# Two-layer network on one core: where the second batch's routing stands in the order against the first batch's last layers

## Chip, cores and metric

The kernel runs on one core of a Trainium2 chip. The metric is the device time of one execution, in microseconds; lower is better. The kernel before took 4369.77 us, the median of three executions (4367.19 to 4371.41).

## What is computed

Four batches of 384 channels by 32 x 32 pixels (1024 tokens) go through two layers, all in float32. Layer 0 is a selective scan in four directions (a recurrence over the tokens with 16 states for each channel), then a mixture of experts: each token picks two of four FFNs of 384 to 1536 to 384. Layer 1 is attention with eight heads and shared q, k and v, then an FFN with Kronecker-structured weights. Cut to what matters:

```python
x = x + scan(ln_c(x))                 # layer 0: four directions, 16 states
t = tokens(x)
t = t + moe(ln_t(t))                  # softmax gate, top 2 of 4 experts
x = from_tokens(t)
x = x + attention(ln_c(x))            # layer 1: softmax(w w^T) w, projection out
t = tokens(x)
t = t + gelu(ln_t(t) @ w_fc.T) @ w_proj.T   # w_fc, w_proj: kron of small matrices
return from_tokens(t)
```

Batches do not depend on each other.

## The kernel before

**Scan.** `scan_layer` walks over 32 units: for each of four batches, four directions, and in each two halves of 512 tokens. `project` prepares the next unit (x_proj, dt, softplus) while `chunk` computes the current one. A unit has three channel blocks `c` of 128 channels, and each four groups `g` of states: 12 steps. In a step POOL multiplies dt*u by B into `bx` (L438, twice) and one half of h by C (L466), ACT computes exp(dt*A) into `da` (L447, four times), DVE runs the recurrence (L452, four times) and multiplies the other half by C (L459, twice), and PE sums the states into the PSUM tile `acc` (L473, four matmuls, each of which the profile counts twice). `bx` has six buffers of which a step takes two; `dtr`, loaded by SP (L422), has seven. At the end of a batch `finish` normalises, applies Gelu, adds the input (POOL, L235) and stores `x1[b]`.

**Tail.** Everything behind the scan is done batch by batch. `between(b)` is called when the scan of batch b has been emitted, and emits `tail_batch(b - 1)`; batch 3 has its tail after the scan. A tail consists of
- `route` and `spread`: load x1, transpose and score it on PE (`tt_ps`, L654), copy (ACT, L640), statistics (DVE, L641, L660, L661), store it as tokens, then `places`: some 60 small DVE instructions that rank the experts and give every token two rows (its counting matmuls at L751 and L752); then the tokens are loaded again, normalised, and scattered with 16 indirect DMAs from POOL's queue (L681) into `rows`, which `clear` has filled with zeros;
- `experts`: 11 slots of gathered rows, each with a load of weights (L869 to L881), a gather (`xs`, L897), transposes (`xc_ps`, L908, copied by DVE at L912), and two products (L925, L940);
- `combine` and `prologue`: 16 indirect gathers on POOL (L970), gate weights, residual, layer norm;
- `attention`: s_ps (L1049), exp on ACT (L1055), o_acc (L1095), and a division by the sums at the end (L1063 to L1076);
- `last_layers`: loads wa, wb, wc and xt (L1119 to L1135), adds the bias on POOL (L1136), projects out into `o_ps` (L1142; DVE L1145 to L1147 add it, and form the FFN's small input), transposes that (`z_ps`, L1164), runs the FFN (`h_ps` L1180, Gelu L1189, `f_acc` L1197) and stores `out` (L1217).

**Order.** A scheduler puts the emitted instructions of each engine into one fixed order at build time, by priority (the order of emission) and a timeline of its own. Blocks under `high_priority(offset=FORWARD)` are taken as if they had been emitted 20,000 instructions earlier, so that they slip between the scan's instructions. `last_layers` and `spread` are such blocks; `attention` and `experts` are not. In the tail of batch b, `second_layer` is given a function that emits the routing of batch b + 1. Tails share one `Room` of buffers: `k4` (five), `kw` (eight), `k12` (two), and four PSUM banks (`o` one, `p` three). On the machine each engine takes its instructions in this order, and waits on semaphores.

Of the kernel before, what the change touches and what calls it, by code (L numbers as in the profile page):

```python
# [114 lines left out]
class Body:  # L115
# [393 lines left out]

    def second_layer(self, b, xc, room, between):  # L510
        att = self.attention(xc, self.sums[:, b], room)
        between()
        with self.tc.high_priority(offset=FORWARD):
            self.last_layers(b, att, room)

    def overflow(self, room):

        nc = self.nc
        flag = self.const.tile([1, 1], I32, tag="flag", name="flag")
        top = room.tile([P, 1], "top", "top")  # L520
        nc.vector.tensor_reduce(
            top, self.sums.rearrange("p b t m i -> p (b t m i)"), AX.X, ALU.max
        )
        ps = room.bank("p", "top_ps")
        nc.tensor.matmul(ps[:1, :P], top, self.ident, start=True, stop=True)
        nc.vector.tensor_reduce(top[:1, :], ps[:1, :P], AX.X, ALU.max)
        nc.vector.tensor_scalar(flag, top[:1, :], LIMIT, None, op0=ALU.is_gt)
        return flag
# [925 lines left out]
```

## Time and profile before

| | |
|---|---|
| median of three executions | 4369.77 us |
| the profiled execution | 4344.16 us, span 4342.4 us |
| granted TensorE clock, mean | 0.857 |
| POOL busy | 3049.3 us (70%) |
| PE busy | 3303.7 us (76%) |
| DVE busy | 2915.6 us (67%) |
| ACT busy | 2504.3 us (58%) |
| DMA engines, mean rate | 160 GB/s |
| POOL's last scan multiply ends | 3487.4 us |

How to read it: the profile lists the busy time of each engine as a share of the span, and cuts the span into forty equal slices whose busy share is given in tenths (9 stands for 90% or more; PEclk is the clock that TensorE was granted). The times by stage give, for a stretch of time, each engine's busy us and, in brackets, its number of instructions. In a group of instructions the columns are busy time and the mean ns of one, then the engine's idle time before them and what ended it. In a wait, the columns are total us, times, and the longest one. "L473" is a line of the kernel before.

### The profile page before, as it was taken

The numbers are of one execution on the slowest core, as the hardware profiler recorded it, in microseconds if no ns is written. First come the engines' busy times: TensorE is split into PE (matmuls) and PEld (weight loads), VectorE is DVE, ScalarE is ACT, GpSimd is POOL, SyncE is SP. The second block draws the span as 40 slices with busy tenths as digits, with TensorE's granted clock in tenths as the row PEclk, the third lists the DMA queues.
The fourth block names the chain that finished last, engine by engine and source line by source line (L and its number), as shares of the span: only waits on it lengthen the run. The fifth ranks groups of instructions, "written<-read, shape, count | busy, mean of one in ns | idle before, by whom it ended". The sixth has DMA issues, their size and how long they took to land. (4 is left out here: it accounts for less than half of the span.)

```text
span 4342.4 us, 45822 instructions
## 1 busy us (share of the span) xinstructions
PE 3303.7 (76%) x13340; PEld 1577.5 (36%) x13340; DVE 2915.6 (67%) x4331; ACT 2504.3 (58%) x4460; POOL 3049.3 (70%) x1475
## 2 busy tenths in 40 slices
PE   6444454398987885679986887569987889998896
PEld 2111111155552222245553222235554235666323
DVE  5999997887787868878886778967877730200101
ACT  5555555466665775467665776466665664343353
POOL 5999997798888968789998688778988820000100
PEclk8666666599998996789998999779998899999897
DMA  5444564567795535458888434457789443335200
GB/s 142 129 119 127 142 160 120 180 196 233 220 281 151 151 118 147 145 161 241 228 242 246 137 107 124 136 149 223 214 237 268 121 147 107 116 127 210 64 17 16
DMA packets 410131, 694.49 MB, mean 160 GB/s; under 512 B 50832, under 2 KB 209424, under 8 KB 409872
## 3 DMA queue, kind: packets, MB, share of 16 engines
q1 hardware_dynamic: 400560, 665.07, 53.6%
q0 software_dynamic: 8192, 25.17, 1.8%
q8 instruction: 107, 1.75, 0.2%
q14 instruction: 152, 1.25, 0.1%
q10 hardware_dynamic: 1120, 1.24, 0.1%
HBM read 569.79 MB, written 121.50 MB: 159 GB/s over the span
## 5 line engine op out<-in xcount | busy, mean ns | idle before, releaser
L438 POOL TENSOR_TENSOR bx<-dtr,bcs 128x1024 f32<-128x1024 f32 x768 | 1795.1, 2364 | 216.2 <-PE acc L473 103.2
L447 ACT ACTIVATE da<-dtr,nega 128x512 f32<-128x512 f32 x1536 | 1045.2, 690 | 994.2 <-DVE bx L459 628.9
L466 POOL TENSOR_TENSOR bx<-bx,bcs 128x1024 f32<-128x1024 f32 x384 | 905.2, 2362 | 160.3 <-DVE carry L463 67.3
L473 PE MATMUL acc<-bx,sel 128*32 128x512 f32 x3072 | 499.2, 702 | 342.4 <-POOL bx L466 273.7
L925 PE MATMUL h_ps<-xc,w 128*128 128x256 f32 (+1 forms) x3168 | 659.5, 363 | 52.0 <-DMA w<-in_w 27.0
L940 PE MATMUL y_ps<-w,hs 128*128 128x384 f32 x1824 | 649.6, 509 | 57.5 <-ACT hs L933 43.6
L925 PEld LDWEIGHTS h_ps<-xc,w 128*128 128x128 f32 x3168 | 547.6, 196 | 219.9 <-issue 92.3
L452 DVE TENSOR_TENSOR_SCAN bx<-da,carry,bx 128x512 f32<-128x512 f32 x384 | 474.0, 1269 | 140.4 <-POOL bx L438 79.5
L452 DVE TENSOR_TENSOR_SCAN bx<-da,bx 128x512 f32<-128x512 f32 x384 | 453.2, 1210 | 107.7 <-ACT da L447 61.7
L452 DVE TENSOR_TENSOR_SCAN da<-da,carry,bx 128x512 f32<-128x512 f32 x384 | 476.9, 1274 | 62.7 <-ACT da L447 51.8
L459 DVE TENSOR_TENSOR bx<-da,bcs 128x512 f32<-128x512 f32 x768 | 509.5, 679 | 3.1
L452 DVE TENSOR_TENSOR_SCAN da<-da,bx 128x512 f32<-128x512 f32 x384 | 455.7, 1219 | 76.0 <-ACT da L447 54.9
L940 PEld LDWEIGHTS y_ps<-w,hs 128*128 128x128 f32 x1824 | 353.6, 198 | 346.0 <-issue 75.7
L1055 ACT ACTIVATE ex<-s_ps 128x512 f32<-128x512 f32 x512 | 300.1, 590 | 157.1 <-PE s_ps L1049 156.1
L1049 PE MATMUL s_ps<-w 64*128 64x512 f32 x1024 | 309.9, 666 | 54.5 <-ACT ex L1055 53.8
L1095 PE MATMUL o_acc<-ex,vt 128*64 128x512 f32 x1024 | 285.6, 637 | 32.9 <-ACT ex L1055 23.5
L473 PEld LDWEIGHTS acc<-bx,sel 128*32 128x32 f32 x3072 | 77.0, 116 | 640.9 <-POOL bx L466 386.6
L930 ACT ACTIVATE hs<-h_ps,bb 128x256 f32<-128x256 f32 (+1 forms) x528 | 199.9, 439 | 185.3 <-PE h_ps L925 180.6
L961 POOL TENSOR_TENSOR diag<-ident,g_weight 128x1024 f32<-128x1024 f32 x8 | 15.1, 1899 | 326.9 <-DMA w<-in_w 312.1
L944 DVE TENSOR_TENSOR y<-y_ps,bb 128x384 f32<-128x384 f32 x76 | 41.7, 549 | 259.0 <-PE y_ps L940 259.0
L363 PE MATMUL dt_ps<-xd,wdt 108*128 108x512 f32 x192 | 123.9, 732 | 73.3 <-ACT mag L402 43.9
L1049 PEld LDWEIGHTS s_ps<-w 64*128 64x128 f32 x1024 | 83.5, 192 | 254.2 <-ACT ex L1055 202.3
(214 smaller groups left out, 3688.4 us busy)
## 6 DMA issues: line engine op xcount, KB each, us to landing
w<-in_w SPq DMA_DIRECT2D x352, 576.0 KB
dtr<-dd SPq DMA_DIRECT2D x1536, 128.0 KB
bcs<-both SPq DMA_DIRECT2D x512, 128.0 KB
dd<-one_e SPq DMA_DIRECT2D x96, 256.0 KB
dd<-mag SPq DMA_DIRECT2D x96, 256.0 KB
rows<-zero SPq DMA_DIRECT2D x76, 192.0 KB
xs<-rows SPq DMA_DIRECT2D x32, 384.0 KB
made<-y SPq DMA_DIRECT2D x32, 384.0 KB
```

Source lines behind the costliest of these rows:

```text
L438: pool = nc.gpsimd.tensor_mul(bx, dtr[q][1], bc[:, 0].unsqueeze(1).to_broadcast([P, 2, HF])).ins
L447: nc.scalar.activation(da, dtr[q][0][:, j, :], AF.Exp, scale=nega[:, col : col + 1])
L452: nc.vector.tensor_tensor_scan(run(h), run(da), run(bx[:, j, :]), 0.0 if first else hold, ALU.mult, ALU.add,)
L459: dve = nc.vector.tensor_mul(bx[:, j, :], h, cg).ins
L466: pool = nc.gpsimd.tensor_mul(bx, bx, cg.unsqueeze(1).to_broadcast([P, 2, HF])).ins
L473: nc.tensor.matmul(acc[lo : lo + DB, :], sel, out[q][:, j, :], start=(g == 0), stop=(g == NG - 1),)
L925: nc.tensor.matmul(ps[:, r, :], w1[(f + r) // wf][:, c, (f + r) % wf * P : ((f + r) % wf + 1) * P], xc[:, c, :], start=(c == 0), stop=(c = ...
L930: nc.scalar.activation(hs[:, f + r, :], ps[:, r, :], AF.Identity, bias=bb[:, f + r : f + r + 1])
L940: nc.tensor.matmul(out[:, :D], hs[:, f, t * P : (t + 1) * P], w2[f // wf][:, f % wf, :], start=(f == 0), stop=(f == FC - 1),)
L1049: ins = nc.tensor.matmul(ps, w[rows, j * P : (j + 1) * P], w[rows, halves(i)], start=True, stop=True).ins
L1055: done.append(nc.scalar.activation(ex[:, o, :], ps, AF.Exp, scale=HD**-0.5, accum_out=sums[:, t, 2 * j + o, i : i + 1],).ins)
L1095: ins = nc.tensor.matmul(out[cols, :], made[t][1][:, j, cols], ex[:, o, :], start=(j == 0), stop=(j == MB - 1),).ins
```

## The change

In `second_layer`, for the first batch alone, the call that emits the second batch's routing is put behind `last_layers` of the first batch; for the other batches it stays ahead of it.

```diff
     def second_layer(self, b, xc, room, between):
         att = self.attention(xc, self.sums[:, b], room)
-        between()
+        if b > 0:
+            between()
         with self.tc.high_priority(offset=FORWARD):
             self.last_layers(b, att, room)
+        if b == 0:
+            between()
```

`between` is the function that `tail_batch` passes. It calls `route(1, ...)` for b = 0, `route(2, ...)` for b = 1 and nothing for b = 2; for batch 3 it is empty. No instruction is added or taken away. Behind the edit each line of the kernel has a number higher by three.

## Prediction

> **What bounds the kernel now.** I read the page first (busy shares, then the forty slices), then the busy times by stage, then the waits of single engines in the stages that the change touches.
>
> ```profile
> PE 3303.7 (76%) x13340; PEld 1577.5 (36%) x13340; DVE 2915.6 (67%) x4331; ACT 2504.3 (58%) x4460; POOL 3049.3 (70%) x1475
> PE   6444454398987885679986887569987889998896
> DVE  5999997887787868878886778967877730200101
> POOL 5999997798888968789998688778988820000100
> PEclk8666666599998996789998999779998899999897
> ```
>
> There are two regimes. Up to about slice 32 (3487 us, where POOL's last scan multiply ends) POOL and DVE share the scan and are both at 7 to 9 tenths. After it PE alone is full: the last batch's layers and the rest of the third's. The chain of waits that ends last lies wholly in that second part, so the time is the end of the scan plus about 855 us. The change touches neither the scan's work nor the end's; it can only move the end of the scan, or the amount of tail work left behind it.
>
> I cut the scan into its 32 units (batch, direction, half), each ending with POOL's 36th multiply, and each unit into 12 steps of four sums into acc. The change bears on units 16, 17 and 18 (steps 180 to 216). The busy times by stage, in order: these three, four undisturbed units under expert work, the regime after the scan:
>
> ```profile
> core 0: us, PE busy (x) PEld busy (x) DVE busy (x) ACT busy (x) POOL busy (x), PEclk, DMA share, GB/s
> 1517.70:1653.30 135.60, 110.80 (x452) 33.85 (x448) 97.24 (x124) 94.56 (x211) 99.17 (x44) 0.91 0.42 125
> 1653.30:1774.60 121.30, 68.01 (x220) 28.94 (x220) 108.21 (x217) 59.53 (x96) 97.17 (x48) 0.71 0.47 130
> 1774.60:1900.20 125.60, 73.58 (x300) 27.44 (x300) 92.04 (x128) 82.14 (x115) 106.61 (x60) 0.68 0.47 149
> 1900.20:2301.20 401.00, 370.94 (x1647) 232.62 (x1648) 338.47 (x458) 268.94 (x427) 364.33 (x170) 0.97 0.85 237
> 3487.00:4342.00 855.00, 763.92 (x3199) 398.10 (x3197) 111.21 (x298) 369.52 (x784) 51.93 (x40) 0.93 0.31 102
> ```
>
> An undisturbed unit takes 401.0 / 4 = 100.25 us. Our three take 382.5, so 82 us hang on the batch boundary, the routing and the last layers. In the second DVE is the bound (108.2 of 121.3), in the third POOL (106.6, the scatter's 16 indirect DMAs among it). PE has half its time free: that PE's order moves is worth nothing by itself; what counts is where DVE's small work lies, and who stands in a queue behind a late wait.
>
> **What the Trainium skill says.** PSUM — Partial Sum Buffer, "Engine vs sequencer instructions": matmuls start and complete in program order, and the queues of ScalarE, VectorE and GpSimdE are strict FIFO. The trace agrees: PE stood 12.5 us before z_ps (L1164) for DVE's z, with sums of the scan behind it. SBUF — State Buffer, "Who interferes with whom": a DVE instruction with two SBUF inputs contends with a GpSimd instruction that reads SBUF, and the one that comes second blocks. The trace shows this strongly. The same 128x32 addition, in the first batch's routing (beside a busy POOL) and in the second's (beside a POOL that waits for DVE):
>
> ```profile
> L665 DVE TENSOR_TENSOR sc<-sc,bg 128x32 f32<-128x32 f32 x1 | 2.3, 2273 | 0.0
> ...
> L665 DVE TENSOR_TENSOR sc<-sc,bg 128x32 f32<-128x32 f32 x1 | 0.2, 182 | 0.0
> ```
>
> **The change, part by part.** No instruction is added or removed. The built order of instructions (it carries no times) shows what moves.
>
> *Projection out and FFN go forward.* The eight o_ps groups stood at steps 199 to 202 on PE and now stand at 187 to 191; the FFN ends at step 203 instead of 212. Its loads wa, wb (step 191 of SP) and wc (195) keep their place, and so does POOL's 6.7 us addition L1136 (step 187); only its six stores of out go forward on SP, from 215-219 to 204-211. On DVE one group is these four, plus 0.16 for its statistics:
>
> ```profile
> L1146 DVE TENSOR_TENSOR o_ps<-xt,wb 128x384 f32<-128x384 f32 x8 | 9.4, 1180 | 0.0
> L541 DVE BATCH_NORM_STATS2 st<-xt 128x6 f32<-128x384 f32 x8 | 4.4, 547 | 0.0
> L1145 DVE TENSOR_TENSOR xt<-xt,o_ps 128x384 f32<-128x384 f32 x8 | 4.3, 534 | 0.3 <-PE o_ps L1142 0.3
> L1147 DVE TENSOR_REDUCE zt<-o_ps 128x32 f32<-128x384 f32 x8 | 4.3, 533 | 0.0
> ```
>
> That is 1.18 + 0.55 + 0.53 + 0.53 + 0.16 = 2.95 us a group. Five of eight groups now fall before step 192: 14.8 us more for DVE in unit 16, less 3.5 for four tiles of routing (L641, L660, L661: 0.86 each) that leave: +11.3. Is there room?
>
> ```profile
> 1625.00:1653.30 28.30, 15.12 (x86) 7.82 (x86) 26.54 (x41) 16.09 (x28) 24.63 (x11) 0.75 0.52 158
> 1653.30:1700.00 46.70, 25.07 (x78) 8.61 (x79) 38.27 (x63) 26.27 (x39) 45.27 (x23) 0.65 0.61 157
> 1700.00:1774.60 74.60, 42.94 (x144) 20.33 (x143) 69.94 (x155) 33.26 (x57) 51.90 (x26) 0.75 0.38 113
> ```
>
> In the last 28.3 us of unit 16 DVE is busy for 26.5 (finish's layer norm lies there), so no: I take +11 for unit 16 (bounds 0, if it fits into DVE's 38 idle us earlier in the unit, and +15). Unit 17 loses those 14.8 and 9.7 of routing and gains some 6 of z and fc1's copy: DVE 108.2 - 24.5 + 6 = 90. The three groups left (8.9) lie in 1653-1700, where DVE has 8.4 free. POOL's 97.2 becomes the bound; with the idle share of an undisturbed unit (POOL 364.3 of 401.0, 9%) that is 107, with PE's stop at z_ps, which stays, 110: -11 (bounds -21, the undisturbed pace, and 0). ACT's Gelu and copies (33 us) go into a unit where ACT is busy for 59.5 of 121: nothing.
>
> *Routing goes back.* Its transposes move from steps 187-196 to 204-205, its two counting matmuls from 199 to 208, its 75 small DVE instructions from 198-206 to 208-211.5, and its scatter on POOL from 206.67 to 212.33. Its four loads and four stores of x (384 KB each) and four loads of xt now stand at 211-212 on SP, behind the stores of out; SP's dtr loads behind them have seven buffers and run about five steps ahead, so I cost this at nothing (bound: one dtr load late, 8 us). The clearing of rows (19 stores, step 175) stays. Now the expert stage's first gather, xc_ps, stands at 212.5 on PE and 213 on DVE, directly behind the scatter; before, seven steps lay between. This form exists in the trace: in the first batch the scatter is at 105.67, xc_ps at 105 and a block of 32 h_ps at 106. That unit shows its price:
>
> ```profile
> 753.40:886.30 132.90, 53.99 (x189) 24.90 (x190) 106.47 (x211) 59.75 (x97) 109.75 (x62) 0.61 0.58 182
> ...
> DVE xc L912 <- PE xc_ps L908: 19.4, 1, 19.4
> ...
> PE xc_ps L908 <- DMA xs<-rows: 16.1, 1, 16.1
> ```
>
> DVE stands 19.4 us at the copy of xc with the scan's instructions behind it, and PE 16.1 for the gathered rows with acc behind it. In unit 18 of before the corresponding waits are 11.1 on PE and 4.5 on DVE. Routing is dearer on DVE, too: 29.0 us in that unit (the groups of its lines summed), 18.9 in the second batch. So unit 18 goes from 125.6 to that unit's 132.9: +7 (bounds -5, if the last layers that leave take more with them, and +20).
>
> *Afterwards.* Expert work starts at step 213 instead of 214, the second batch's attention ends at 295 instead of 300, the third's experts start at 316 instead of 319, but the third's attention starts at step 371 in both. Behind the scan stand 190 matmuls of it instead of 194: four s_ps or o_acc of 0.53 us, -2.
>
> Sum: +11 - 11 + 7 - 2 = +5. The profiled execution took 4344.2 (span 4342.4); the median is 4369.8, 25.6 above. I add the difference to the median: **4375**.
>
> **Rivals.** *Faster:* the last layers vanish into idle time. Unit 16 pays 4, unit 17 falls to 100.25 (-21), unit 18 stays, end -2: -19, 4351. For it: PE's and ACT's slack, and that DVE alone binds unit 17. Against it: the full DVE at 1625-1653, and that separate small work meets a busy POOL and so costs more, as L665 shows; overlapped, two sets of DVE work hide in one stall of POOL.
> *Slower:* one mechanism, the queue behind the scatter. PE stands 16.1 us for xs, then runs 35 h_ps (2 x 0.41 = 0.82 us each, L925 in 866-960) before acc of step 213: 16.1 + 28.6 = 44.7. POOL can run three steps ahead in its six bx buffers, 3 x 7.5 = 22 us; what exceeds that, 22.7, less the 2.9 that POOL waits there now, is 20. It decides from the point where xs comes later than POOL's buffers last. Then +11 - 11 + 20 - 2 = +18, 4388. Against it: in the first batch POOL lost only a few us after the same block, since DVE was behind as well.
> That the change does nothing is excluded by the built order.
>
> **How the numbers follow.** Near +5 (own range -6 to +16): 0.43, of which 0.28 within 0.2% (8.7 us, about what a measurement here can tell from no change) and 0.15 slower. Faster rival 0.27. Slower rival 0.30, of which 0.02 within. So faster 0.27, same 0.30, slower 0.43. The range reaches to both rivals and the ends of the bounds less a tenth on each side: 4347 to 4397.
>
> **What would show it.** Unit 16 longer by some 10 us with DVE full at its end; unit 17 at about 110 with POOL its busiest engine and no o_ps waits on DVE in it; unit 18 at about 133 with waits of DVE at L915 and of PE at L911 (the changed kernel's lines) near 15-20 us; 855 us after the scan's end. Wrong if unit 17 stays at 121 (then DVE did not bind it), if the gathered rows come without a wait, or if the difference lies in units after 20, which I hold equal.

## The result, and the profile after

The kernel after took 4343.82 us, the median of five executions (4342.38 to 4351.83), and the kernel before 4367.19 (4357.68 to 4371.41) beside it: a ratio of 0.9956 (95% interval 0.9939 to 0.9972). Three later comparisons gave 0.9971 (0.9961 to 0.9981), 0.9963 (0.995 to 0.9976) and 0.9971 (0.996 to 0.9982). So the change makes the kernel 0.3 to 0.4% faster, 13 to 19 us by these ratios. (The medians beside each other are 23 us apart in the first comparison and 9 to 12 in the three later ones.) The forecast was 4375, five slower, in a range of 4347 to 4397.

Executions of one kernel in one series on one chip spread over up to 35 us, and the medians of before differ by up to 0.7% between the series (4336.54 to 4367.19), so ratios are always those to the kernel before in the same series. The profile of before that the prediction worked from was a quick execution (4344.16 us beside 4357.68 to 4371.41 in the timed ones); the profiled execution of after took 4343.82 us, and these two spans hardly differ (4342.4 and 4341.5). Where a difference of a few microseconds matters, several profiles of either order are used.

The page of the kernel after, the rows that were shown of before:

```profile
PE 3304.0 (76%) x13340; PEld 1569.6 (36%) x13340; DVE 2909.9 (67%) x4331; ACT 2499.4 (58%) x4456; POOL 3051.7 (70%) x1475
PE   6445444298987887668986886579896889998896
DVE  6999997787887868878887777788887730200101
POOL 5999997798888977888988788788988830000100
PEclk9666666599998997779998998789998899999996
```

Nothing stands out in the sums: the same two regimes, and nearly the same work. The program's own instructions are the same, but ACT has 4456 instead of 4460: it loads its function tables 143 times instead of 147, and its order has changed. Two of the missing four lie behind the scan. The times by stage, cut at the same events (ends of units 16, 17, 18, 22, 27 and 32; columns as before: us, then busy us and instructions of PE, PEld, DVE, ACT and POOL, then PEclk, DMA share, GB/s), say where it moved:

```profile
1520.30:1659.50 139.20, 125.74 (x492) 40.57 (x488) 103.15 (x131) 92.30 (x206) 99.98 (x45) 0.95 0.36 107
1659.50:1783.60 124.10, 79.69 (x265) 25.73 (x268) 100.81 (x162) 85.49 (x120) 98.10 (x48) 0.70 0.37 106
1783.60:1916.00 132.40, 67.33 (x287) 35.03 (x280) 103.54 (x179) 59.56 (x103) 106.49 (x59) 0.69 0.64 192
1916.00:2326.90 410.90, 374.38 (x1652) 231.59 (x1652) 336.02 (x456) 273.89 (x436) 363.01 (x169) 0.95 0.85 240
2326.90:2952.20 625.30, 467.51 (x1881) 176.53 (x1880) 478.39 (x759) 400.75 (x764) 507.33 (x253) 0.86 0.49 144
2952.20:3492.40 540.20, 454.98 (x1907) 248.47 (x1905) 423.95 (x567) 342.49 (x579) 470.64 (x225) 0.91 0.72 206
3492.40:4341.50 849.10, 754.83 (x3179) 392.94 (x3177) 109.42 (x295) 365.04 (x779) 51.61 (x39) 0.93 0.30 102
```

The fifth row has this counterpart in the kernel before:

```profile
2301.20:2943.00 641.80, 462.27 (x1870) 173.42 (x1869) 484.98 (x755) 407.17 (x777) 506.44 (x254) 0.85 0.52 147
```

The scan loses time in units 16 to 22 and gets most of it back in units 23 to 27. What is left is behind the scan: PE does 3179 matmul records there instead of 3198, in 849.1 us instead of 855.0. The same table from more profiles, those of the experiments below included (seven with the order of before up to step 371, five with the order of after up to step 380; means, in us):

| stage | before | after | difference | forecast |
|---|---|---|---|---|
| unit 16 | 135.6 | 139.9 | +4.3 | +11 |
| unit 17 | 121.1 | 122.5 | +1.4 | -11 |
| unit 18 | 126.4 | 131.0 | +4.6 | +7 |
| units 19 to 22 | 402.8 | 414.0 | +11.1 | 0 |
| units 23 to 27 | 641.6 | 623.6 | -17.9 | 0 |
| units 28 to 32 | 541.4 | 540.8 | -0.7 | 0 |
| POOL's last scan multiply (with units 1 to 15) | 3488.0 | 3491.4 | +3.4 | +7 |
| behind it (unaltered tails: four of before, five of after) | 857.6 | 845.5 | -12.1 | -2 |
| the same, brought to one granted clock (see below) | 854.4 | 846.6 | -7.8 | -2 |

The profiles of the stretch behind the scan were 855.0, 865.5, 855.5 and (with Exp for Gelu in the first batch's FFN, which leaves the tail as it is) 854.3 us for before; 849.2, 846.5, 846.1, 846.1 and (with the same Exp) 839.7 for after. The two sets don't overlap. Those of the scan's end do: 3480 to 3500 and 3487 to 3498.

Part of the spread in either set is the clock that TensorE was granted in that stretch. The four tails of before have the same order on PE, and in the order of the list the traces give them 0.932, 0.923, 0.930 and 0.934: the longest tail has the lowest clock. Length times clock is the same within 0.5% in the four (795.5 to 799.0), while the lengths differ by 1.3%. The five of after had 0.931, 0.935, 0.933, 0.933 and 0.939 (788.4 to 791.8). So an estimate of the lengths at one clock, 0.9333 (that of the last profile of the unchanged kernel after), is 852 to 856 us for before and 845 to 848 for after: by this estimate about 8 us of the difference are the order, and the rest is the clock of the executions that happened to be profiled.

### The profile page after: what moved, and what is told of

It reads as the page before. It is cut to its first block, busy times and chain, and to the rows that moved or that the text cites. A ratio compares the mean times of both kernels' runs of the same rounds, so it can differ in the third digit from the quotient of the medians.

```text
span 4341.5 us, 45836 instructions
## 1 busy us (share of the span) xinstructions
PE 3304.0 (76%) x13340; PEld 1569.6 (36%) x13340; DVE 2909.9 (67%) x4331; ACT 2499.4 (58%) x4456; POOL 3051.7 (70%) x1475
## 5 line engine op out<-in xcount | busy, mean ns | idle before, releaser
L473 PE MATMUL acc<-bx,sel 128*32 128x512 f32 x3072 | 516.6, 709 | 337.7 <-POOL bx L466 272.3
```

The costliest lines, as they stand in the source:

```text
L473: nc.tensor.matmul(acc[lo : lo + DB, :], sel, out[q][:, j, :], start=(g == 0), stop=(g == NG - 1),)
```

## The experiments

My first theory, from the first pair of profiles, was that the order behind the scan gives the gain; its rival was that the scan itself becomes shorter and that the profile of before, a quick execution, hides it.

**Both kernels again, and the edit at other batches.** The two kernels unchanged, and two other placements of the routing. A third version, with `between()` behind the last layers for b = 0 and b = 1:

```diff
-        between()
         with self.tc.high_priority(offset=FORWARD):
             self.last_layers(b, att, room)
+        between()
```

and a fourth with it behind them for b = 1 alone (`if b != 1: between()` ahead, `if b == 1: between()` behind).

> The kernel before, unchanged, to see which execution its profile shows. Theory A (before's executions differ among themselves, and its first profile at 4344 was a rare quick one): the times lie at 4357 to 4371 again, and a new profile near 4365 shows units that took longer than in the first one by some 20 us in all. Theory B (the first profile is typical and the timed runs carry some 23 us more around the program): a new profile near 4344 again, with timed runs near 4367.

> The changed kernel, unchanged, beside the one before on the same chip. Theory A: 4342 to 4352, ratio 0.9956 (0.994 to 0.997), and a profile within 10 us of the first. Theory B: its profile is some 20 us under its timed runs as well.

> The routing behind the last layers for the first and the second batch. If the gain comes from where the routing stands (last layers early, routing alone beside the scan), a second such move brings it again: about 0.991, 4325. If a routing that stands alone costs what I priced (+5 and what the profile shows, +13 over units 16 to 18), and the gain comes from elsewhere, the second move gives it back: 0.9956 to 1.000, 4345 to 4367.

> The routing behind the last layers for the second batch alone; the first keeps the order of before. If the position as such gains, as much as the change: 0.9956, about 4347. If the gain is a matter of the first batch's place in the scan (its waits against the batch boundary), nothing or a loss: 1.000 to 1.004, 4367 to 4385.

Measured: before 1.0002 (0.9992 to 1.0012), after 0.9971 (0.9961 to 0.9981), both batches 0.999 (0.998 to 1.0001), the second alone 1.0007 (0.9996 to 1.0019). The gain is real and belongs to the first batch's edit; the same edit at the next batch takes most of it back. POOL's last multiply ends at 3500.4, 3497.7, 3492.6 and 3488.0 us. The version with the second batch's edit alone ends its scan first and has 870.8 us behind it, with 3279 matmul records; both edits leave 868.4 us, 3277 records. So what sets after apart from before in these profiles is not the end of its scan, but the stretch behind it (846.5 us against 865.5, of which the granted clock explains a part, as said above). The other two show that the two stretches trade: with 80 more records behind the scan, the scan ends 8 to 12 us sooner than that of before, and the total hardly moves.

**The tail held.** If the gain lies behind the scan, it must vanish when both kernels go into the tail alike. In both kernels the third batch's attention from its second head pair on is queued on PE behind the scan's last sum:

```diff
-                    nc.tensor.matmul(
+                    self.last_sum = nc.tensor.matmul(
...
+        self.held = b == 2
         att = self.attention(xc, self.sums[:, b], room)
...
+        def hold(t):
+            if self.held and t >= 1:
+                return self.tc.issue_after(self.last_sum)
+            return nullcontext()
...
-                    made.append(project(t + 1))
+                    with hold(t + 1):
+                        made.append(project(t + 1))
```

(and likewise around the scores and the products with V). The traces show the same order behind the scan in both, on PE, DVE, ACT and POOL; the order within the scan is that of each kernel.

> The order of before, but the third batch's attention from its second head pair on is queued on PE behind the last sum of the scan. Up to step 372 of 384 all orders are those of before; behind the scan they are, on all five engines, the same as in the changed kernel held in the same way. 64 attention matmuls move behind the scan (0.53 us each, up to 34 us if nothing hides them). Theory P (the gain of the change lies in what stands behind the scan's end): the held pair differs by less than 0.15%, and both have the same time behind POOL's last scan multiply within 4 us. Theory S (the gain lies inside the scan): the held changed kernel stays 9 to 16 us ahead.

> The changed kernel, held in the same way; 68 attention matmuls move behind the scan. Theory P: the same time as the held kernel of before, within 6 us. Theory S: 9 to 16 us less than that.

Measured beside before: 1.0074 (1.006 to 1.0088) and 1.0081 (1.0068 to 1.0094). POOL's last multiply at 3464.4 and 3460.8 us; 892.3 and 891.9 us behind it. With the same tail, no gain is left: the two ratios differ by 0.0007, give or take 0.002, where the change gave 0.003 to 0.004. (These are six and five executions.) The pair also prices the tail: 3371 records take 892 us and 3179 take some 847, so 45 us for 192 records, about 0.23 us each, waits included. And it shows that such work is not free beside the scan either: the held kernel of before ended its scan 15 us sooner than the other profile of before's order in that series (3464.4 and 3479.6 us, the second from the next experiment), while its tail was 38 us longer.

**The table loads.** In unit 17 of after, ACT is the suspect (see the next section). Each Gelu of the FFN makes ACT load its table, and load that of Exp again, at 1.28 us a load. In both kernels the first batch's last FFN takes Exp instead of Gelu, which leaves the nonlinearity of this one FFN out. The expectation was that its eight loads go with it. The traces show that only the four of Gelu went (143 loads instead of 147 in before, 139 instead of 143 in after; in unit 17 of after 6 instead of 10), since `exp_again` still asks for the other four:

```diff
-            self.exp_again(nc.scalar.activation(hs, hs, AF.Gelu).ins)
+            self.exp_again(nc.scalar.activation(hs, hs, AF.Gelu if b else AF.Exp).ins)
```

> The kernel before with the same replacement. There the FFN lies in unit 18 (125.6 and 129.4 us): 116 to 121 if ACT's queue matters in it, 125 to 129 if not.

> The changed kernel with Exp in place of Gelu in the first batch's last FFN (its nonlinearity is left out); Exp is in the table set that the scan uses, so that eight table loads of 1.28 us go from ACT, 10.2 us in all, and nothing else moves in any order. If ACT's queue kept unit 17 at 121 to 124 us where I had 110: unit 17 at 110 to 115. If it did not (DVE, or sums waiting for something else): unit 17 within 3 us of 121 to 124. The total follows by at most that, 0 to -10.

Measured: 0.9981 (0.997 to 0.9993) for before and 0.9961 (0.9946 to 0.9975) for after, so the change still gives 0.2% (0.9961 / 0.9981, from four and seven executions). Unit 17 of after took 118.5 us (122.5 on average with the loads, 120.7 to 124.2), unit 18 of before 123.3 (126.4 on average, 125.6 to 129.4). Four loads, 5.1 us of ACT, are worth 3 to 4 us to the unit in which they lie, by one profile each. All eight were not taken out; if the other four are worth as much, which is an estimate, unit 17 would stand near 115, and the loads are not all that kept it from 110.

**The turn of a head pair.** The built orders show what is different at the scan's end. When attention goes from one head pair to the next, PE runs the division of the old one (`bc_ps`), projects the new one (`w_ps`), waits for ACT to copy, transposes (`v_ps`), and makes first scores (`s_ps`). In the kernel after the turn to the third head pair stands at steps 381 and 382, in that of before at 382, and its transposes behind step 384. The theory: this turn is the gain. Three kernels move it, with little else. To bring it into the scan of before, the projections of the second and the third head pair go under high priority (so the second pair's transposes come forward by one or two steps too):

```diff
+        self.early = b == 2
         att = self.attention(xc, self.sums[:, b], room)
...
-                    made.append(project(t + 1))
+                    early_on = self.early and t + 1 <= 2
+                    with self.tc.high_priority(offset=FORWARD) if early_on else nullcontext():
+                        made.append(project(t + 1))
```

To send it out, the hold from above with `t >= 2`, in both kernels.

> The kernel before with one thing changed at its end: the projections of the second and third head pair of the third batch's attention are put under high priority. In the built order their matmuls and transposes then stand ahead of the scan's last sum (the third pair's transposes at steps 382 and 383 instead of behind 384), as in the kernel after; the order of everything up to step 371 is that of the kernel before. The turn theory (the gain is the turn from the second to the third head pair: in the kernel before its transposes, its copies on ACT and its first scores stand just behind the scan's end, in the kernel after within the scan): the stretch behind POOL's last multiply falls from 855 to 865 us to 845 to 850, and the ratio is 0.9965 to 0.998. The rival (the gain comes out of the first batch's shift and its consequences within the scan): ratio 0.9995 to 1.0005.

> The kernel before, with the third batch's attention from its third head pair on queued on PE behind the scan's last sum: only six projection matmuls leave the scan's end, the turn lies wholly behind it. The turn theory: 858 to 872 us behind POOL's last multiply, ratio 1.000 to 1.002. The rival has no view of it beyond the six matmuls: ratio 1.000 to 1.001.

> The kernel after with the same hold: everything of the changed order up to step 380 stays, only the turn to the third head pair is sent behind the scan's last sum, where the built order is that of the held kernel before. The turn theory: the gain is gone, within 0.1% of the held kernel before, 858 to 872 us behind POOL's last multiply. The rival: it stays 0.3% below the held kernel before (ratio 0.997 to 0.998 beside before).

> The kernel after, unchanged, as the yardstick on this chip: ratio 0.9955 to 0.9975 by both theories, some 847 to 850 us behind POOL's last multiply.

Measured:

| kernel | ratio to before (95%) | POOL's last multiply | behind it | PE records there |
|---|---|---|---|---|
| before, turn in | 0.9985 (0.9976 to 0.9994) | 3486.3 | 844.9 | 3196 |
| before, turn out | 0.9994 (0.9982 to 1.0007) | 3480.0 | 854.1 | 3199 |
| after, turn out | 1.0012 (0.9998 to 1.0026) | 3487.0 | 856.4 | 3191 |
| after | 0.9963 (0.995 to 0.9976) | 3491.1 | 846.1 | 3179 |

The stretch behind the scan follows the turn, whichever the rest of the order: 845 and 846 us with the turn in, 854 and 856 with it out (2 to 4 us less than I had expected of the latter). The granted clock there was 0.939, 0.934, 0.930 and 0.933 in the order of the table; at the one clock used above these are about 850 us for before with the turn in, 855 and 854 with it out, and 846 for after. So the turn is worth 4 to 8 us of the tail, less than the plain lengths say. These rows are of before with the turn in, and of after with the turn out:

```profile
3486.30:4331.20 844.90, 756.06 (x3196) 394.79 (x3194) 110.19 (x296) 369.15 (x783) 51.59 (x40) 0.94 0.31 103
```

```profile
3487.00:4343.40 856.40, 765.35 (x3191) 398.19 (x3191) 109.69 (x295) 369.16 (x784) 51.56 (x40) 0.93 0.31 102
```

The time of after loses its gain with the turn out; by its ratio it even lies 0.18% above before with the turn out, though the intervals touch, so whether the hold costs after something besides the turn is open. And before with the turn in gained only 0.15%, less than the theory's 0.2 to 0.35%, and less than after. Was the turn all of it?

**Three orders in one series, and another way in.** Before, after, and before with the turn in, profiled and timed together; and before with the whole attention of the third batch under high priority:

```diff
-        att = self.attention(xc, self.sums[:, b], room)
+        with self.tc.high_priority(offset=FORWARD) if b == 2 else nullcontext():
+            att = self.attention(xc, self.sums[:, b], room)
```

> The kernel before, unchanged, profiled beside the next three. Both theories: ratio 0.999 to 1.001, and 853 to 866 us behind POOL's last multiply.

> The kernel after, unchanged. Ratio 0.9955 to 0.9975, 845 to 850 us behind POOL's last multiply. If the turn is all of the gain, POOL's last multiply ends within 5 us of that of the kernel before, or later; if the scan itself gains, it ends 5 to 10 us earlier.

> The kernel before with the turn to the third head pair within the scan, as in the earlier run of it (two projections under high priority). If the turn is all of the gain: ratio 0.9965 to 0.998, within 0.1% of the kernel after. If the turn is about half of it: 0.998 to 0.9992, and 0.1 to 0.25% above the kernel after.

> The kernel before with the whole attention of the third batch under high priority: another way to bring the turn into the scan (the third head pair's transposes at steps 382 and 383), with the routing of the fourth batch and the FFN of the third as before. If the turn is all of the gain: 845 to 850 us behind POOL's last multiply, ratio 0.9965 to 0.998. If half of it: 0.998 to 0.9992.

Measured: before 1.0005 (0.999 to 1.002), after 0.9971 (0.996 to 0.9982), turn in 0.9987 (0.9976 to 0.9998), whole attention 0.998 (0.9969 to 0.9992). POOL's last multiply ended at 3490.9, 3489.0, 3486.5 and 3484.7 us, and 855.5, 846.1, 847.8 and 838.3 us lay behind it. By the profiles, then, after gains 9.4 us behind the scan and 1.9 ahead of its end, and the turn in gives before 7.7 us behind the scan. At one clock (0.930, 0.933, 0.933 and 0.941 were granted behind the scan) these are about 6 and 4 us, and 8 for the whole attention. By the times the turn in gives 0.13 and 0.15%, and the whole attention, which moves more than the turn, 0.2%, of the 0.3 to 0.4%. So bringing the turn in gives two fifths to a half of the gain, and the whole attention two thirds, by ratios whose intervals are wide. The other 4 to 10 us (the ratios of 0.9985, 0.9987 and 0.998 against those of after beside them; the medians give 1 to 7) show in the times alone: over all profiles, the scan of after ends no earlier.

One thing on record goes with that rest. In the three later series the executions of after had a mean granted clock 0.0015 to 0.002 above those of before (0.8568 and 0.8553, 0.8596 and 0.8579, 0.8601 and 0.8581). Among before's own executions in these series the time falls by 2.0 to 2.5 us for each 0.001 of that clock (a straight line through 59, 43 and 67 executions; it is loose, correlations of -0.47 to -0.58). That makes 3 to 4 us. Whether the new order draws the higher clock, or something else raises both, was not tried. The rest stays open.

## Why the prediction was wrong, step by step

**Where the turn was overlooked.** The step that failed is the end of "Afterwards": 190 matmuls of attention behind the scan instead of 194, four of 0.53 us, -2. The place was right, the size was not: it measured -12 by the plain means and about -8 at one granted clock. The scan itself came out at +3.4 for a forecast of +7. I counted scores and products by kind, and left out what else moves with them at that point: a projection, its transposes, and the wait for ACT that a turn contains. In the traces 20 records of attention fewer begin behind POOL's last multiply (19 in the rows, which count those under way at the border too): 8 of transposes (`v_ps`), 6 of the projection (`w_ps`), and only 6 of the kinds that I had counted (`s_ps`, `o_acc`). The premise "that PE's order moves is worth nothing by itself" was read from units 16 to 18; at the scan's end it fails, where bringing the turn forward gave 0.13 and 0.15%. This is PE at the turn, in the profiles of before and of after from the last series (start, us, operation, idle time before it). POOL's last multiply ends at 3490.9 us in the first, 3489.0 in the second. The last two rows are the whole stretch behind it in each:

```profile
3486.58 1.92 PE L1071 MATMUL bc_ps<-ident,inv 128*64 128x128 f32 x32
3488.43 2.84 PE L1026 MATMUL w_ps<-xc,wqkv 128*128 128x512 f32 x6
3491.20 1.08 PE L1095 MATMUL o_acc<-ex,vt 128*64 128x512 f32 x4
3492.21 2.84 PE L1026 MATMUL w_ps<-xc,wqkv 128*128 128x512 f32 x6
3494.99 1.92 PE L473 MATMUL acc<-bx,sel 128*32 128x512 f32 x16
3496.84 1.09 PE L1035 MATMUL v_ps<-ident,w 128*128 128x128 f32 x8
```

```profile
3477.23 1.97 PE L1074 MATMUL bc_ps<-ident,inv 128*64 128x128 f32 x32
3479.12 2.84 PE L1029 MATMUL w_ps<-xc,wqkv 128*128 128x512 f32 x6
3481.90 1.08 PE L1098 MATMUL o_acc<-ex,vt 128*64 128x512 f32 x4
3482.91 2.84 PE L1029 MATMUL w_ps<-xc,wqkv 128*128 128x512 f32 x6
3485.68 1.06 PE L473 MATMUL acc<-bx,sel 128*32 128x512 f32 x8
3486.67 0.66 PE L1038 MATMUL v_ps<-ident,w 128*128 128x128 f32 x4
```

```profile
3490.90:4346.40 855.50, 764.34 (x3198) 398.27 (x3197) 110.82 (x297) 369.53 (x784) 51.55 (x40) 0.93 0.31 102
3489.00:4335.10 846.10, 757.03 (x3179) 396.32 (x3177) 109.29 (x295) 364.59 (x779) 51.50 (x39) 0.93 0.31 102
```

The turn begins 4.3 us ahead of the scan's end in before, and 11.8 in after: 7.5 us. Over the whole tail PE is busy for 764.3 us in the first and 757.0 in the second (-7.3), and idle for 91.2 and 89.1 (-2.1): together the 9.4. While the scan runs, PE has idle time in which it waits for POOL and DVE, so work that it does there is cheap, though not free, as the held pair shows (15 us of scan for 38 of tail); behind the scan's end PE alone sets the pace, and each record costs its 0.23 us. Nineteen records are some 4.4 of the 7.3 us. The other 2.9 are about what the granted clock gives: behind the scan it was 0.36% higher in the second (0.930 and 0.933), and 0.36% of 764.3 us is 2.7.

Why the third batch's attention is a step ahead in after was not tried. The order shows only that its second head pair's transposes stand at step 372 instead of 375 on PE, though the attention starts at 371 in both. The link from the edit in the first batch to this place is therefore shown by its effect, and not explained.

**Units 16 and 17: the split was wrong, and the sum 6 us too low.** I had +11 and -11; it was +4.3 and +1.4, so the move that was to cancel out cost 5.7. DVE is full to the end of unit 16, as forecast, and stays full for 40 us of unit 17:

```profile
1630.00:1659.50 29.50, 28.69 (x122) 14.63 (x122) 29.46 (x45) 11.74 (x18) 22.54 (x11) 0.94 0.27 78
1659.50:1700.00 40.50, 25.57 (x60) 9.43 (x60) 39.95 (x65) 16.60 (x25) 25.13 (x13) 0.75 0.32 92
1700.00:1783.60 83.60, 54.12 (x206) 16.30 (x208) 60.85 (x97) 68.89 (x96) 72.97 (x36) 0.68 0.39 114
```

From 1700 us on DVE has time (60.85 of 83.6) and POOL too, while ACT is busy for 68.89. That is the FFN, whose work on ACT I costed at nothing in this unit because ACT had half its time free. PE waited for its output 20.1 us in three pieces:

```profile
PE f_acc L1200 <- ACT hs L1192: 20.1, 3, 10.6
```

A wait of PE in the FFN holds the scan's sums behind it, and ACT's own queue holds the scan's Exp behind the Gelu. Four of the eight table loads are 3 to 4 us of the unit by experiment (this wait was then 16.0 us); how the rest divides between ACT's queue and the DVE work that slipped in from unit 16 was not tried. It is the case named as wrong in the prediction ("if unit 17 stays at 121 (then DVE did not bind it)"): DVE's busy time fell from 108.2 to 100.8 us (90 were forecast), and the unit did not follow.

**Unit 18: the right number by another way.** Forecast 132.9, measured 132.4 (131.0 on average, against 126.4). But PE stood 6.0 us for the gathered rows, not 16.1, and DVE 3.4 us at the copy of xc, not 19.4. In their place stood the preparation of the next unit (first row: a wait of PE; second: of DVE, ended by something the profile does not show):

```profile
PE acc L473 <- ACT mag L402: 25.9, 2, 17.1
...
PE xc_ps L911 <- DMA xs<-rows: 6.0, 1, 6.0
```

```profile
DVE dt_ps L400 <- issue: 16.7, 1, 16.7
...
DVE xc L915 <- PE xc_ps L911: 3.4, 1, 3.4
```

Pricing a stage by a stage of the same kind (the first batch's) gave its length well and its mechanism badly. The routing was nearly as dear as that comparison said: the 128x32 addition, 182 ns in before, took 1581 ns beside a busy POOL. Over the lines of `route`, `spread` and `places` DVE was busy for 25.9 us in this unit, against 18.9 for the same work in before; the comparison gave 29.0.

```profile
L668 DVE TENSOR_TENSOR sc<-sc,bg 128x32 f32<-128x32 f32 x1 | 1.6, 1581 | 0.0
```

It began 0.8 us into a multiply of POOL and ended 0.05 us behind that multiply's end. This agrees with what the Trainium skill says in SBUF — State Buffer, "Who interferes with whom": a DVE instruction with two inputs in SBUF contends with a GpSimd instruction that reads SBUF.

**Units 19 to 27: held equal, but were not.** They moved by +11.1 and -17.9. In the last series, the second batch's experts ran from 1895.9 to 2327.9 us in after, and from 1905.2 to 2344.7 in before: begun 9 us earlier, while the scan was 12 us later at the end of unit 18, so more of their work lies beside units 19 to 22, and less beside unit 23 (118.6 us instead of 127.7). At the next batch boundary the last layers of the second batch end at 2873 instead of 2909 us, and unit 27, in which they lay, falls from 131.9 to 107.7. This is read from the traces and was not tried. Most of it cancels: what leaves one unit is paid for in another. The whole scan moved by +3.4 us, where +7 was forecast, and both lie within the spread of the profiles.

**The rivals.** The faster one gave 4351 and came nearest in time, but not in cause: the last layers did not vanish into idle time, and unit 17 stayed far from 100 us. The queue behind the scatter did not form: PE stood 6 us for the rows, and POOL stood 7.5 us for PE in unit 18 (2.9 before), where the rival had 20 more.

**The median.** I added 25.6 us, by which the profiled execution was quicker than the median, to the sum. An offset of one execution is no property of the kernel: the later profiles of before took 4367.7 us against a median of 4363.05, and 4348.2 against 4341.4. Without it the sum was 4349.2, and the profiled execution of after took 4343.8. That this comes near is luck: the executions of before beside it took 4367.19, and the sign of the forecast was wrong all the same. The offset belongs into the range, on both sides.

## What to carry to other kernels

When a kernel has a stage that one engine fills, behind stages in which that engine has time to spare, look first at what a reordering anywhere ahead moves across that border: count every operation behind it, of all kinds, with its waits, and price it at that engine's pace; what it moves within the earlier stage may come back two stages later. Test such a claim by making both kernels enter the last stage alike, and by moving only the piece at the border. And before a difference of 0.5% is read from two profiles, take more of them, and compare the clock that each was granted in the stretch in question: here it made up 3 of the 9 us between two of them. Count in the trace, too, whether an experiment took out what it was meant to take out.

## What the runs showed of the hardware that was not expected

The same kernel's executions spread over 4319 to 4354 us in 43 executions of one series on one chip, with one core in use; its medians differed between the series by up to 0.7%, and the gain of 0.3 to 0.4% held in all four in which it was measured. Behind the scan, the length of the same order times its granted clock was the same within 0.5% in four profiles, though the clock went from 0.923 to 0.934. The addition into PSUM of 128x384 (L1149 after, L1146 before) took 1137 ns on average in unit 16, 1837 ns in unit 17 of the same execution, and 560 behind the scan, where POOL is busy for 52 of 849 us. What POOL did beside it was not varied.
